# An encoder's softmax heads: VectorE scales the last head of every second group and adds it to the third, and residual additions move behind the maximum

## The chip, the core and the metric

The kernel runs on one core of a Trainium2 chip. A core has four engines that matter here, each with its own in-order queue of instructions: TensorE (PE in the profile; its weight loads are PEld), VectorE (DVE), ScalarE (ACT) and GpSimd (POOL). A fifth, SyncE (SP), issues most DMA transfers. Matrix products and transposes land in PSUM, from which VectorE and ScalarE read. Engines wait for each other through semaphores. The metric is the device time of one execution in microseconds.

## What is computed

The reference chains four blocks over a sequence of 2 batches x 1024 positions x 128 features, each with a layer norm before it and a residual addition behind it: a Mamba block, a mixture of experts, a six-layer encoder, and a feed-forward block with FP4 rounding. The change touches the encoder alone. One of its layers:

```python
scores = jnp.einsum('blhd,bmhd->bhlm', q, k) * inv_sqrt_d      # 16 heads of size 8
w_avg = jax.nn.softmax(scores, axis=-1).mean(axis=1)           # mean over the heads
new_w = jax.nn.softmax(CSCALE * w_avg + rel[None], axis=-1)    # second softmax
sa = jnp.einsum('blm,bme->ble', new_w, h)
h1 = _ln(h + sa, l1w, l1b)
h2 = _ln(h1, l2w, l2b)
ff = jax.nn.relu(h2 @ w1.T + b1_) @ w2.T + b2_
return (_ln(h2 + ff, l3w, l3b), None)
```

For each block of 128 query rows, sixteen softmax matrices of 128 x 1024 are averaged. Since the average is a sum, the heads may be added in any order and by any engine.

## The kernel before

The encoder does 6 layers x 2 batches x 8 blocks of 128 rows x 16 heads = 1536 steps, one head of one row block each. The method run (L1067) writes the order of all four engines' instructions by hand, step by step; no scheduler moves them. In step s it issues, in this order:

- release (L1098): if a piece of feed-forward work has a result waiting in PSUM, the instruction that takes it out (on ScalarE, or for the second feed-forward product the addition L926 on VectorE);
- in one step of sixteen, residual (L1057): VectorE takes a reciprocal of the second softmax's sum (L1062) and adds the mixed values to the layer's input (L1063). Every fourth such residual also puts the layer's norms, feed-forward and next projection (between, L885) on the list of work, in pieces;
- scores (L947): PE computes 128 x 1024 scores in two matmuls (L963) into PSUM, and VectorE takes their negated maximum (L966);
- in one step of four, scaled (L981): VectorE takes the reciprocals of four heads' softmax sums (L986), and GpSimd multiplies each of the four heads' exponentials by its reciprocal, in place in SBUF (L989), one instruction of 128 x 1024 a head;
- added (L991): for a group of four heads whose scores were issued ten steps before, PE transposes scaled exponentials onto two accumulators in PSUM (L1008). A group takes four steps: two heads' first halves, the other two heads' first halves, and then the same for the second halves. Each step is eight transposes of 128 x 128, and PSUM adds them up over the 16 heads;
- in two steps of sixteen, shifted (L1018) adds the distance term to the mean on VectorE (L1022), and second (L1032) takes its exponential on ScalarE (L1035);
- exponentials (L969): ScalarE takes the head's exponential and its sum (L972), from PSUM into one of 13 SBUF tiles;
- in one step of sixteen, mixed (L1043): PE multiplies the second softmax with the layer's input (L1048). In the other steps one piece of the listed work is issued.

Scores, the mixed values and all feed-forward results share three PSUM buffers (L668, L706). A score matmul can start when ScalarE has taken the exponential of an earlier user of its buffer. VectorE meets its instructions strictly in the order above: a maximum cannot start while an instruction issued ahead of it waits.

The GpSimd queue holds the scalings and, between them, products and additions of layer norms (L781 to L805), the addition L900, and the splitting of queries and keys into bfloat16 parts (L847, L849).

Of the kernel before, what the change touches and what calls it, by code (L numbers as in the profile page):

```python
# [14 lines left out]
ALU = mybir.AluOpType  # L15
# [13 lines left out]
NL, NH, DH, FF = 6, 16, 8, 512  # L29
# [605 lines left out]
class Encoder:  # L635
# [345 lines left out]
    def scaled(self, a, s):  # L981

        nc = self.nc
        m, hh = divmod(s, NH)
        rz = self.small.tile([P, self.GT], F32, tag="rz", bufs=4, name=f"rz_{a['who']}_{s}")
        nc.vector.reciprocal(rz, a["z", m][:, hh : hh + self.GT])  # L986
        for i in range(self.GT):
            e = a["e", s + i]
            nc.gpsimd.tensor_scalar(e, e, rz[:, i : i + 1], 1.0, ALU.mult, ALU.mult)  # L989

    def added(self, a, s, i):  # L991

        m, hh = divmod(s, NH)
        if hh == 0 and i == 0:
            a["acc", m] = [
                self.psa.tile([P, 4, P], F32, tag=f"acc{k}", name=f"acc_{a['who']}_{m}_{k}")
                for k in range(2)
            ]  # L1000
        half, two = divmod(i, 2)
        for j in (2 * two, 2 * two + 1):
            e = a["e", s + j]
            if half:
                del a["e", s + j]
            for n in range(4):
                at = (4 * half + n) * P
                self.nc.tensor.matmul(  # L1008
                    a["acc", m][half][:, 3 - n, :],
                    e[:, at : at + P],  # L1010
                    self.c.ident,
                    is_transpose=True,
                    start=hh + j == 0 and n == 0,
                    stop=hh + j == NH - 1,
                    skip_group_check=True,
                )

# [49 lines left out]
    def run(self):  # L1067
        th = self.TH
        drain(self.layer(0))
        for b in range(B):  # L1070
            self.hn[b] = self.hidden(b, f"in_{b}")
            for half in range(2):
                hs = slice(half * th, half * th + th)
                src = self.x[:, b * TB : (b + 1) * TB, :][:, hs, :]
                drain(self.norm(self.hn[b][:, hs, :D], src, f"c0_{b}_{half}"))
        for half in range(2):
            drain(self.project(0, 0, half))
        steps = TB * NH
        n = NL * B * steps
        lag, gt = self.LAG, self.GT  # L1080
        atts = {}
        work = []

        def add(b, pieces):
            work.append([b, pieces, None])

        def advance(i):

            if i >= len(work):
                return False  # L1090
            try:
                work[i][2] = next(work[i][1])
                return work[i][2] is not WAIT
            except StopIteration:
                del work[i]
                return False

        def release():  # L1098

            for i in range(len(work)):  # L1100
                if work[i][2] is HOLD:
                    advance(i)
                    return

        def of(s):
            return atts[s // steps], s % steps

        for half in range(2):
            add(1, self.project(0, 1, half))
        for s in range(n + lag + gt + 6):  # L1110
            release()

            t = s - lag - gt - 4
            if t >= 0 and t % NH == NH - gt:
                a, ts = of(t)
                m = ts // NH
                self.residual(a, m)
                if m % th == th - 1:
                    add(a["b"], self.between(a["l"], a["b"], m // th))
            if s < n:  # L1120
                if s % steps == 0:
                    i = s // steps
                    while any(b == i % B for b, _, _ in work):
                        advance(0)
                    atts[i] = self.begin(i)
                    if i % B == B - 1 and i // B + 1 < NL:
                        work.insert(0, [None, self.layer(i // B + 1), None])
                self.scores(*of(s))
            if s % gt == 1 and gt < s <= n + 1:
                self.scaled(*of(s - gt - 1))  # L1130
            t, i = divmod(s - lag, gt)
            t *= gt
            last = 0 <= t < n and t % NH == NH - gt and i % 2
            if 0 <= t < n:
                self.added(*of(t), i)
                if last:
                    a, ts = of(t)
                    self.shifted(a, ts // NH, i // 2)
            if s < n:
                self.exponentials(*of(s))  # L1140
            if last:
                self.second(a, ts // NH, i // 2)
            t = s - lag - gt - 3
            if t >= 0 and t % NH == NH - gt:
                a, ts = of(t)
                self.mixed(a, ts // NH)
            else:
                first = 1 if s % 4 == 3 and len(work) > 1 else 0
                if not advance(first):
                    advance(1 - first)  # L1150
        while work:
            advance(0)


def drain(pieces):
    for _ in pieces:
        pass
# [190 lines left out]
```

## Time and profile before

Three runs took 3608.43, 3609.01 and 3609.79 us (median 3609.01).

| | us |
|---|---|
| time of the profiled execution | 3610.56 |
| its span, first to last instruction | 3608.5 |
| PE busy | 3077.6 (85%) |
| VectorE busy | 2652.2 (73%) |
| ScalarE busy | 2494.5 (69%) |
| GpSimd busy | 2520.3 (70%) |
| the encoder's heads, first to last maximum | 669 to 3384 |
| mean granted TensorE clock | 0.917 of full speed |

How to read the lines that follow. A group's line names source line, engine, operation, the tiles written and read, the shape and the count; behind the first bar come busy time in us and the mean length of one instruction in ns; behind the second the idle time of the engine just ahead of these instructions, and what ended most of it. A line of the timeline has the start in us, the length in us, engine, source line, tiles, shape and how many instructions it merges; square brackets hold idle time ahead of it. A line of a window has start and end, the length, and the busy time of PE, PEld, VectorE, ScalarE and GpSimd in it, with instruction counts in brackets, then the granted clock, the DMA share and GB/s. Since PE's instructions are pipelined and their ends are modelled, start-to-start times say more about PE than its busy time.

### The profile page before, as it was taken

What the parts mean: (1) busy time and instruction counts of PE and PEld (TensorE: products, weight loads), DVE (VectorE), ACT (ScalarE), POOL (GpSimd) and SP (SyncE); (2) the same over time, 40 slices, a digit from 0 to 9 for tenths busy, and PEclk for the clock granted to TensorE, in tenths of its full rate; (3) what the DMA queues carried; (4) which work ended last, traced back from release to release, by engine and by line L of the source; (5) the groups of instructions that cost most, each with busy time, mean ns of one, the idle gap of its engine ahead of it and who ended that gap; (6) DMA issues with size and microseconds to landing.
All of it is one profiled execution on the core that took longest, in us unless ns stands there. A gap on an engine that the chain in (4) does not pass through costs nothing. (4 is left out here: it accounts for less than half of the span.)

```text
span 3608.5 us, 56501 instructions
## 1 busy us (share of the span) xinstructions
PE 3077.6 (85%) x20551; PEld 2409.3 (67%) x20551; DVE 2652.2 (73%) x4250; ACT 2494.5 (69%) x4506; POOL 2520.3 (70%) x2791
## 2 busy tenths in 40 slices
PE   5656997688999999899999999999999999999735
PEld 2345664376777777777777777777777777777513
DVE  6887434476887787787877778877778777778488
ACT  4553334476888888777887777877788777878532
POOL 3997001666887888777887778877788777877532
PEclk8656998799999999999999999999999999999856
DMA  2453001311111121111201111111111111110000
GB/s 80 116 133 90 1 1 26 81 14 23 35 29 36 20 51 22 30 39 16 49 24 29 35 20 42 31 30 33 21 40 27 25 35 20 38 18 8 1 7 11
DMA packets 124043, 125.09 MB, mean 35 GB/s; under 512 B 13459, under 2 KB 102372, under 8 KB 120308
## 3 DMA queue, kind: packets, MB, share of 16 engines
q1 hardware_dynamic: 122900, 118.82, 15.7%
q8 instruction: 162, 2.65, 0.3%
q0 software_dynamic: 864, 2.66, 0.2%
q14 instruction: 117, 0.96, 0.1%
HBM read 101.25 MB, written 20.19 MB: 34 GB/s over the span
## 5 line engine op out<-in xcount | busy, mean ns | idle before, releaser
L966 DVE TENSOR_REDUCE nm<-sc 128x1 f32<-128x1024 f32 x1536 | 1851.6, 1218 | 433.4 <-PE sc L963 394.5
L972 ACT ACTIVATE e<-sc,nm 128x1024 f32<-128x1024 f32 x1536 | 1703.9, 1112 | 521.5 <-DVE nm L966 380.7
L989 POOL TENSOR_SCALAR e<-e,rz 128x1024 f32<-128x1024 f32 x1536 | 1690.6, 1120 | 504.9 <-DVE rz L986 461.2
L1008 PEld LDWEIGHTS acc<-ident,e 128*128 128x128 f32 x12288 | 1465.1, 142 | 344.1 <-POOL e L989 35.3
L1008 PE MATMUL acc<-ident,e 128*128 128x128 f32 x12288 | 1636.3, 276 | 14.9 <-POOL e L989 14.9
L963 PE MATMUL sc<-k,q 72*128 72x512 bf16 x3072 | 939.5, 387 | 164.9 <-ACT e L972 112.4
L963 PEld LDWEIGHTS <-q 72*128 72x128 bf16 x3072 | 305.5, 100 | 299.5 <-issue 272.1
L972 ACT ACTIVATION_READ_ACCUMULATOR e<-sc,nm 128x1 f32 x1536 | 297.8, 194 | 0.0
L286 PE MATMUL ys<-ident,yc 128*128 128x128 f32 x512 | 113.3, 382 | 105.8 <-POOL yc L418 88.5
L581 ACT ACTIVATE hT<-ph,b 128x512 f32<-128x512 f32 x128 | 88.0, 687 | 135.9 <-PE ph L574 133.6
L286 PEld LDWEIGHTS ys<-ident,yc 128*128 128x128 f32 x512 | 84.4, 196 | 142.3 <-POOL yc L418 107.2
L615 POOL TENSOR_TENSOR x<-fo,x 128x512 f32<-128x512 f32 x4 | 5.1, 1278 | 235.6 <-DVE fo L94 235.6
L598 DVE SCALAR_TENSOR_TENSOR eo<-po,hot,eo 128x128 f32<-128x128 f32 x256 | 71.9, 344 | 132.7 <-PE po L590 127.4
L1048 PE MATMUL sa<-h,prT 128*128 128x129 f32 x1280 | 161.6, 280 | 8.6 <-ACT e L972 7.3
L1048 PEld LDWEIGHTS sa<-h,prT 128*128 128x128 f32 x1280 | 153.6, 195 | 11.9 <-ACT e L972 11.1
L369 POOL TENSOR_TENSOR db<-dtx,bb 128x512 f32<-128x512 f32 x128 | 159.6, 1266 | 0.2
L590 PEld LDWEIGHTS po<-m_w,hT 128*128 128x128 f32 x1024 | 125.1, 195 | 30.6 <-ACT hT L581 15.7
L1035 ACT ACTIVATE prT<-mean,zero 128x512 f32<-128x512 f32 x192 | 137.0, 714 | 8.2 <-DVE mean L1022 8.2
L356 ACT ACTIVATE da<-dt,zero,na 128x512 f32<-128x512 f32 x128 | 99.8, 781 | 55.0 <-DVE hh L402 51.3
L1022 DVE SCALAR_TENSOR_TENSOR mean<-acc,rel 128x512 f32<-128x512 f32 x192 | 128.8, 671 | 11.6 <-PE acc L1008 11.5
L590 PE MATMUL po<-m_w,hT 128*128 128x128 f32 x1024 | 127.3, 278 | 0.0
L793 ACT ACTIVATE r<-r,v_c,r_c 128x128 f32<-128x128 f32 x192 | 83.4, 484 | 47.3 <-POOL v_c L788 47.3
(313 smaller groups left out, 2808.9 us busy)
## 6 DMA issues: line engine op xcount, KB each, us to landing
bb<-bcd SPq DMA_DIRECT2D x128, 256.0 KB
q<-d_bq SPq DMA_DIRECT2D x432, 64.0 KB
k<-d_bk SPq DMA_DIRECT2D x144, 192.0 KB
d_bq<-part_bq SPq DMA_DIRECT2D x72, 128.0 KB
d_bk<-part_bk SPq DMA_DIRECT2D x72, 128.0 KB
e_W<-in_L_attn_W SPq DMA_DIRECT2D x12, 256.0 KB
m_w<-in_L_ffn_W POOLq DMA_DIRECT2D x2, 1024.0 KB, 11.0
e_ln_w<-in_L_attn_ln_w SPq DMA_DIRECT2D x18, 64.0 KB
```

Of the source, the lines that this page charges most:

```text
L286: nc.tensor.matmul(ys[k][:, t, :], src[:, t * P : (t + 1) * P], c.ident, is_transpose=True, start=first and t == 0, stop=last, skip_group_ ...
L356: nc.scalar.activation(da[g, k], dt[b][:, k, halves[h]], AF.Exp, bias=c.zero, scale=na[:, k, j : j + 1],)
L369: nc.gpsimd.tensor_mul(db[g, k], dtx[b][:, k, halves[h]], bb[g][:, 0, :])
L590: nc.tensor.matmul(po[:, m, :], hT[:, k, m * P : (m + 1) * P], t["w2"][:, e, k, :], start=k == 0, stop=k == NHC - 1,)
L963: nc.tensor.matmul(sc[:, ss], q, qk["kt"][hh // self.GH][:, hh % self.GH, ss], start=True, stop=True)
L966: nc.vector.tensor_reduce(a["nm", m][:, hh : hh + 1], sc, AX.X, ALU.max, negate=True)
L972: self.nc.scalar.activation(e, a.pop(("sc", s)), AF.Exp, bias=a["nm", m][:, hh : hh + 1], accum_out=a["z", m][:, hh : hh + 1],)
L989: nc.gpsimd.tensor_scalar(e, e, rz[:, i : i + 1], 1.0, ALU.mult, ALU.mult)
L1008: self.nc.tensor.matmul(a["acc", m][half][:, 3 - n, :], e[:, at : at + P], self.c.ident, is_transpose=True, start=hh + j == 0 and n == 0, ...
L1022: self.nc.vector.scalar_tensor_tensor(t, a["acc", m][half].rearrange("p n q -> p (n q)"), 1.0 / NH, self.rel[:, at : at + self.HL], ALU.mu ...
L1035: self.nc.scalar.activation(t.rearrange("p n q -> p (n q)"), a.pop(("mean", m, half)), AF.Exp, bias=self.c.zero,)
L1048: self.nc.tensor.matmul(sa[:, : D + 1], prT[n // 4][:, 3 - n % 4, :], a["h"][:, n, :], start=n == 0, stop=n == TB - 1,)
```

## The change

In every second group of four heads, GpSimd scales only three heads, in the order third, first, second. Two steps after the group's reciprocals, VectorE multiplies the fourth head's exponentials by its reciprocal and adds them to the third head's scaled exponentials, in place: one scalar_tensor_tensor of 128 x 1024 with both tensors in SBUF. PE then transposes three heads of that group instead of four, so the group's second and fourth steps have four transposes each instead of eight.

Besides, release and the residual move from the head of the step to behind the scores, so on VectorE they stand behind the step's maximum; what puts the next work on the list is one step later than before.

```diff
-        for i in range(self.GT):
+        heads = [0, 1, 2, 3]
+        if self.merges(s):
+            heads = [2, 0, 1]
+            a["rz", s] = rz
+        for i in heads:
             e = a["e", s + i]
             nc.gpsimd.tensor_scalar(e, e, rz[:, i : i + 1], 1.0, ALU.mult, ALU.mult)
+
+    def merges(self, s):
+        return s // self.GT % 2 == 1
+
+    def merged(self, a, s):
+        if self.merges(s):
+            e = a["e", s + 2]
+            self.nc.vector.scalar_tensor_tensor(
+                e, a.pop(("e", s + 3)), a.pop(("rz", s))[:, 3:4], e, ALU.mult, ALU.add
+            )
...
-        for j in (2 * two, 2 * two + 1):
+        n_heads = self.GT - self.merges(s)
+        for j in range(2 * two, min(2 * two + 2, n_heads)):
...
-                    stop=hh + j == NH - 1,
+                    stop=hh + self.GT == NH and j == n_heads - 1,
...
         for s in range(n + lag + gt + 6):
-            release()
-
-            t = s - lag - gt - 4
+            t = s - lag - gt - 5
             if t >= 0 and t % NH == NH - gt:
                 a, ts = of(t)
                 m = ts // NH
-                self.residual(a, m)
                 if m % th == th - 1:
                     add(a["b"], self.between(a["l"], a["b"], m // th))
...
                 self.scores(*of(s))
+            release()
+            t = s - lag - gt - 4
+            if t >= 0 and t % NH == NH - gt:
+                a, ts = of(t)
+                self.residual(a, ts // NH)
             if s % gt == 1 and gt < s <= n + 1:
                 self.scaled(*of(s - gt - 1))
+            if s % gt == 3 and gt < s <= n + 3:
+                self.merged(*of(s - gt - 3))
```

## The prediction

> **What bounds the kernel now.** I read the page's busy table first, then the stretch in which the encoder's heads run (from the first maximum to the last), then the groups.
>
> ```profile
> span 3608.5 us, 56501 instructions
> ...
> 669.00:3384.00 2715.00, 2518.72 (x18036) 2040.55 (x18035) 2112.20 (x2943) 2143.67 (x3865) 2149.15 (x2407) 0.97 0.15 29
> ```
>
> The second line has start and length of the stretch, then busy time of PE, PEld, DVE, ACT and POOL, the granted clock, the DMA share and GB/s. The reader is to see that the encoder is three quarters of the span, that PE is busy 93% of it, and DVE, ACT and POOL each 78 to 79%.
>
> ```profile
> L966 DVE TENSOR_REDUCE nm<-sc 128x1 f32<-128x1024 f32 x1536 | 1851.6, 1218 | 433.4 <-PE sc L963 394.5
> ...
> L989 POOL TENSOR_SCALAR e<-e,rz 128x1024 f32<-128x1024 f32 x1536 | 1690.6, 1120 | 504.9 <-DVE rz L986 461.2
> L1008 PEld LDWEIGHTS acc<-ident,e 128*128 128x128 f32 x12288 | 1465.1, 142 | 344.1 <-POOL e L989 35.3
> L1008 PE MATMUL acc<-ident,e 128*128 128x128 f32 x12288 | 1636.3, 276 | 14.9 <-POOL e L989 14.9
> ```
>
> VectorE's main idle time is waiting for PE's scores. Next the timeline of PE, in a calm place, gives a head's true price there:
>
> ```profile
> 1848.79 1.04 PE L1008 MATMUL acc<-ident,e 128*128 128x128 f32 x8
> 1849.67 0.60 PE L963 MATMUL sc<-k,q 72*128 72x512 bf16 x2
> 1850.10 1.04 PE L1008 MATMUL acc<-ident,e 128*128 128x128 f32 x8
> ```
>
> From score to score is 1.31 us, of which eight transposes hold 0.88 (1849.67 - 1848.79), so 0.11 each. VectorE's maxima behind each other start 1.13 us apart (two of them took 2.36 us at 1857.11, one 1.22). So PE leads VectorE by only 0.18 us a head in calm places; it is the clear bound only where feed-forward matmuls lie between the heads. Busy time by row of 16 heads shows this (columns as above; four rows are one half of a batch's layer, 64 heads):
>
> ```profile
> 1792.86:1818.33 25.47, 24.58 (x190) 20.68 (x189) 22.16 (x34) 21.64 (x43) 18.92 (x23) 1.00 0.37 63
> 1818.33:1845.07 26.74, 25.21 (x184) 20.19 (x183) 21.39 (x32) 22.21 (x41) 23.52 (x24) 1.00 0.06 20
> 1845.07:1870.88 25.81, 23.65 (x178) 19.30 (x177) 22.20 (x32) 21.68 (x38) 24.79 (x30) 1.00 0.15 35
> 1870.88:1903.80 32.92, 29.60 (x198) 23.30 (x197) 21.83 (x26) 25.54 (x46) 23.68 (x27) 0.95 0.01 3
> ```
>
> VectorE's idle time (length less busy) is 3.31, 5.35, 3.61 and 11.09 us. Over the encoder it is (2715.0 - 2112.2) / 96 rows = 6.28, against 5.84 here, so I scale by 1.075: 4.4 us in each of three light rows, about 11.9 in the heavy one.
>
> **The change part by part, for a row of 16 heads (96 rows).**
>
> *TensorE, removed.* Two groups of four lose one head's transposes: 16 x 0.11 = 1.76 us; 169 us over the kernel if PE alone set the pace. By the mean of the group's busy time (1636.3 / 12288 = 0.133) it would be 204 us, the upper bound of any gain; the lower is nothing, where VectorE sets the pace. I take 0.11, which is start to start.
>
> *GpSimd, removed.* 192 scalings of 1.120 us, 215 us. Its idle time is (2715.0 - 2149.2) / 96 = 5.9 us a row, and what waits for it on PE's side is 14.9 + 35.3 us in all, so this alone buys little. The order in the group becomes third, first, second head; PE reads the group's first two heads five heads after the reciprocal was issued, so 1.12 us of delay is hidden by about 8 us.
>
> *VectorE, added.* 192 scalar_tensor_tensor of 128x1024 with both tensors in SBUF. The same shape runs in the Mamba stage (L220 below) in 1.279 us. The bounds are 1.19 (instructions behind each other overlap by 0.09) and 1.285 (the longest of twelve). I take 1.28: 246 us, 2.56 a row. Per head the engine is then near PE: PE's 1.31 x 8 - 0.88 = 9.6 us for eight calm heads, VectorE's 1.13 x 8 + 1.2 + 0.2 for two reciprocals = 10.4.
>
> *VectorE, the wait that the merge adds.* It is issued two maxima behind the group's reciprocal, and needs only the third head's scaling, which GpSimd does first. But GpSimd is then in its second or third scaling. What the trace shows of VectorE reading two SBUF tensors beside a busy GpSimd:
>
> ```profile
> L220 DVE SCALAR_TENSOR_TENSOR cv<-xp,cw,cv x12: 1276/1279/1285, 40.2 to 58.3; 128x1024 f32<-128x1024 f32 x12
> ...
> L274 DVE SCALAR_TENSOR_TENSOR w<-w,u x8: 692/1596/5852, 66.7 to 198.5; 128x512 f32<-128x512 f32 x8
> ...
> L275 DVE SCALAR_TENSOR_TENSOR w<-ps_dt,w x8: 691/691/692, 67.5 to 200.1; 128x512 f32<-128x512 f32 x8
> ...
> 91.20 2.50 POOL L369 TENSOR_TENSOR db<-dtx,bb 128x512 f32<-128x512 f32 x2
> ...
> 92.05 5.85 DVE L274 SCALAR_TENSOR_TENSOR w<-w,u 128x512 f32<-128x512 f32 x1
> ...
> 93.65 1.26 POOL L418 TENSOR_TENSOR yc<-hh,bb 128x512 f32<-128x512 f32 x1
> ...
> 94.87 2.48 POOL L369 TENSOR_TENSOR db<-dtx,bb 128x512 f32<-128x512 f32 x2
> ```
>
> L274 (minimum, median, maximum in ns) and L275 are the same operation and size; only L274 has both tensors in SBUF. L275 always takes 0.69 us, L274 up to 5.85: in the last rows it ends 0.55 us after GpSimd's unbroken run ends at 97.35. In the encoder no VectorE instruction reads two SBUF tensors today (L1022, L1063 and L926 take one from PSUM), so the wait is new. Its bounds are 0 (GpSimd idle, or no exclusion against a one-input scaling) and 5852 - 692 = 5.16 us. For the value I took, in the trace, each second group's reciprocal, the end of the second maximum behind it and the end of the third scaling, which would be GpSimd's last. The scaling ends later in 75% of 191 groups; quartiles of the difference are 0.16, 0.77 and 1.62 us; counting an earlier end as 0, the mean is 1.26. When both start at once it is plain arithmetic: two maxima take 2.5 us, three scalings 3.4. I take 1.2. Other GpSimd work behind the run (layer norm products of 1.27 us, L803 and L805) can lengthen it; a GpSimd one scaling shorter in eight shortens it.
>
> The Trainium skill, page "SBUF — State Buffer", section "Who interferes with whom", speaks against this change: a VectorE instruction with two SBUF inputs and a GpSimd instruction that reads SBUF exclude each other for the whole instruction, and whichever issued first goes on. L274 agrees in kind. Read as a wait for the running scaling only, it would be an estimate of half of 1.12, 0.56 us a merge, and the sum below would come out 16 us faster than before. The rows of L274 show longer waits, through four instruction boundaries, so I keep 1.2.
>
> Queued behind the waiting merge on VectorE is the next head's maximum; ACT's exponential (L972) waits for that, and PE's score three allocations on waits for ACT, since the scores have three PSUM buffers. TensorE's wait for the merged head itself is hidden: it is read four heads later, about 6.5 us.
>
> *Moved.* The residual (L1062, 169 ns, and L1063, 351) and the feed-forward additions (L926, 292 ns) go behind the maximum. Before, they fell into the 0.6 us in which PE makes the next scores, so VectorE lost little; now they follow the maximum and the next may start up to 0.5 us later, 96 x 0.5 + 96 x 0.3 = 77 us if nothing hides it. Below nothing: the maximum need no longer wait behind L1062's 133.8 us of waiting, at most that. I take 0, because where VectorE lags, order leaves its sum as it is. The evacuations on ACT stay between the same exponentials. The feed-forward pieces, GpSimd work and DMA issues on SP included, start one head later; a batch's layer has 128 heads, so I count nothing. GpSimd's and SP's queues gain nothing else.
>
> *Sum.* A row asks VectorE for 2 x (1.28 + 1.2) = 4.96 us more. I let 1.0 us of idle stay (the wait at the row's mixing matmul, about 1.5 us, is partly used). Light row: 4.96 - (4.4 - 1.0) = +1.56. Heavy row: the merge fits, and PE's 1.76 is gained, less some for its first calm heads: -1.2. Four rows: 3 x 1.56 - 1.2 = +3.48; 24 such fours: +84 us. On the profiled execution's own 3610.56 us (span 3608.5 and 2.1 around it) that is 3694; the median is 1.55 lower, so 3693.
>
> **The rivals.**
> *Faster: no wait.* If GpSimd's scaling, with one input, does not exclude the merge, or leaves it in at a boundary, w = 0: light rows 2.56 - 3.4 = -0.84, heavy -1.76, 24 x -4.28 = -103, 3506 us. With w the light row is 2.56 + 2w - 3.4, and with -1.5 in the heavy row the sum is zero at w = 0.67 us; that decides. For it: all eight waits of L274 are against two-input instructions. Against: 75% of the runs end too late.
> *Much slower: the merge waits until GpSimd has emptied its queue*, layer norm products included: w = 2.5, light rows 7.56 - 3.4 = +4.16, heavy 7.56 - 10.9 < 0, say -0.5: 24 x 12 = +288, 3897 us. For it: the 5.85. Against: in three of L274's eight, VectorE got in between two instructions.
> *No change:* w near 0.67, 3609.
>
> **How the numbers follow.** Forecast 55% (3630 to 3790 its own range, w from 0.8 to 1.7), faster rival 25%, much slower 15%, no change 5%. The measurement can tell about 0.2%, 7 us. Below 3545 lies about half of the faster rival, above 3830 half of the much slower: a fifth in all. So faster 0.25, same 0.05, slower 0.70.
>
> **What would show it.** Merges with a mean over 2 us and a spread up to 4 or more, ending about 1.3 us after a GpSimd run's end; GpSimd's idle time up, PE's too; calm rows near 27.5 us, heavy ones shorter by about 1. Merges at 1.28 throughout would prove me wrong, as would light rows that stay at 26 with merges near 2.5: then VectorE's idle time was more usable than I think.

## The result and the profile after

The changed kernel takes 3742.36 us (median of 4 runs, 3739.87 to 3743.40) against 3608.72: a ratio of 1.0370, 95% interval 1.0352 to 1.0388. The change costs 134 us. The forecast was 3693 us, 84 slower.

The page of the changed kernel, its first line, and the stretch of the encoder's heads (start and end, length, busy time of PE, PEld, VectorE, ScalarE and GpSimd, granted clock, DMA share, GB/s):

```profile
span 3738.2 us, 53054 instructions
...
668.30:3514.40 2846.10, 2486.41 (x16513) 1905.67 (x16512) 2353.85 (x3134) 2149.37 (x3865) 2036.14 (x2215) 0.96 0.15 28
```

The encoder takes 2846 us instead of 2715; the rest of the kernel is as long as before. TensorE is busy 32 us less, GpSimd 113 less, VectorE 242 more. TensorE's share falls from 93 to 87%; VectorE's rises from 78 to 83%. No engine is full: each now waits more for the others. The page's groups say who waits (busy time and mean length, then idle time and what ended it, as in the prediction):

```profile
L966 DVE TENSOR_REDUCE nm<-sc 128x1 f32<-128x1024 f32 x1536 | 1828.5, 1212 | 467.7 <-PE sc L963 462.7
L972 ACT ACTIVATE e<-sc,nm 128x1024 f32<-128x1024 f32 x1536 | 1705.1, 1112 | 682.4 <-DVE nm L966 561.2
L993 POOL TENSOR_SCALAR e<-e,rz 128x1024 f32<-128x1024 f32 x1344 | 1550.6, 1171 | 743.9 <-DVE rz L986 715.0
...
L1024 PE MATMUL acc<-ident,e 128*128 128x128 f32 x10752 | 1484.6, 279 | 21.4 <-POOL e L993 21.4
```

ScalarE's wait for the maxima has grown from 381 to 561 us. VectorE's own wait for the scores, instead of shrinking, has grown from 395 to 463. Both fit one loop: scores, maximum, exponential, and the exponential frees the PSUM buffer for a later score. In the list of waits, TensorE's scores waiting for ScalarE rise from 112 to 241 us. The same four rows of 16 heads as in the prediction:

```profile
1857.63:1887.59 29.96, 25.20 (x183) 19.84 (x182) 25.33 (x36) 22.29 (x43) 17.93 (x23) 1.00 0.30 54
1887.59:1917.52 29.93, 26.06 (x171) 19.24 (x170) 24.89 (x35) 22.18 (x39) 22.38 (x21) 0.94 0.06 19
1917.52:1946.84 29.32, 25.56 (x164) 19.54 (x162) 24.91 (x36) 21.35 (x38) 23.04 (x27) 0.88 0.18 30
1946.84:1979.35 32.51, 28.34 (x179) 20.91 (x178) 24.13 (x27) 24.95 (x46) 22.79 (x26) 0.95 0.01 3
```

The three light rows are 3.2 to 4.5 us longer than before, the heavy one 0.4 shorter. VectorE's idle time in the light rows is 4.63, 5.04 and 4.41 us, where it was 3.31, 5.35 and 3.61. So in these light rows the merges were simply added; they did not fill idle time. In the heavy row it falls from 11.09 to 8.38, and there a part of them fits.

The merge itself, as all its instructions and as one of them on the timelines of VectorE and GpSimd:

```profile
L1002 DVE SCALAR_TENSOR_TENSOR e<-e,rz,e x192: 1270/1607/2235, 691.4 to 3518.4; 128x1024 f32<-128x1024 f32 x192
...
1799.21 2.33 DVE L966 TENSOR_REDUCE nm<-sc 128x1 f32<-128x1024 f32 x2
1801.87 2.14 DVE L1002 SCALAR_TENSOR_TENSOR e<-e,rz,e 128x1024 f32<-128x1024 f32 x1 [0.33 <-POOL e L993]
1803.93 2.34 DVE L966 TENSOR_REDUCE nm<-sc 128x1 f32<-128x1024 f32 x2
...
1800.71 4.28 POOL L993 TENSOR_SCALAR e<-e,rz 128x1024 f32<-128x1024 f32 x3
1804.96 1.27 POOL L803 TENSOR_TENSOR r<-r,e_ln_w 128x512 f32<-128x512 f32 x1
```

A third of the merges take 1.27 to 1.28 us; the median is 1.61, the longest 2.24, the mean 1.66. The one shown starts as the first scaling ends and the second begins, and takes 2.14. The three scalings beside it take 4.28 us, where three behind each other took 3.31 before: the third ends about a microsecond late, behind the merge. Over the kernel 72 scalings take over 1.2 us, and all 1344 together 71 us more than at 1.118 each.

### The profile page after: what moved, and what is told of

Read it like the earlier page. It is cut to its first block, busy times and chain, and to the rows that moved or that the text cites. A ratio compares the mean times of both kernels' runs of the same rounds, so it can differ in the third digit from the quotient of the medians.

```text
span 3738.2 us, 53054 instructions
## 1 busy us (share of the span) xinstructions
PE 3045.2 (81%) x19015; PEld 2275.7 (61%) x19015; DVE 2892.5 (77%) x4442; ACT 2500.1 (67%) x4506; POOL 2408.0 (64%) x2599
## 5 line engine op out<-in xcount | busy, mean ns | idle before, releaser
L966 DVE TENSOR_REDUCE nm<-sc 128x1 f32<-128x1024 f32 x1536 | 1828.5, 1212 | 467.7 <-PE sc L963 462.7
L993 POOL TENSOR_SCALAR e<-e,rz 128x1024 f32<-128x1024 f32 x1344 | 1550.6, 1171 | 743.9 <-DVE rz L986 715.0
L1024 PEld LDWEIGHTS acc<-ident,e 128*128 128x128 f32 x10752 | 1317.5, 144 | 350.0 <-issue 36.6
L1024 PE MATMUL acc<-ident,e 128*128 128x128 f32 x10752 | 1484.6, 279 | 21.4 <-POOL e L993 21.4
L963 PE MATMUL sc<-k,q 72*128 72x512 bf16 x3072 | 954.9, 393 | 317.3 <-ACT e L972 241.2
L1002 DVE SCALAR_TENSOR_TENSOR e<-e,rz,e 128x1024 f32<-128x1024 f32 x192 | 318.6, 1659 | 42.8 <-POOL e L993 42.8
L1064 PE MATMUL sa<-h,prT 128*128 128x129 f32 x1280 | 170.0, 289 | 6.5 <-ACT e L972 6.0
L1064 PEld LDWEIGHTS sa<-h,prT 128*128 128x128 f32 x1280 | 161.5, 204 | 11.1 <-ACT e L972 10.2
```

The costliest lines, as they stand in the source:

```text
L963: nc.tensor.matmul(sc[:, ss], q, qk["kt"][hh // self.GH][:, hh % self.GH, ss], start=True, stop=True)
L966: nc.vector.tensor_reduce(a["nm", m][:, hh : hh + 1], sc, AX.X, ALU.max, negate=True)
L1002: self.nc.vector.scalar_tensor_tensor(e, a.pop(("e", s + 3)), a.pop(("rz", s))[:, 3:4], e, ALU.mult, ALU.add)
L1024: self.nc.tensor.matmul(a["acc", m][half][:, 3 - n, :], e[:, at : at + P], self.c.ident, is_transpose=True, start=hh + j == 0 and n == 0, ...
L1064: self.nc.tensor.matmul(sa[:, : D + 1], prT[n // 4][:, 3 - n % 4, :], a["h"][:, n, :], start=n == 0, stop=n == TB - 1,)
```

## The experiments

All runs were timed in three rounds against the kernel before on the same chip (its medians 3606 to 3608 us); the ratio follows each time.

**The two halves of the change, apart.** Merge alone, with release and residual where they were (the edit against the changed kernel, the removed lines of the moved order left out):

```diff
-            t = s - lag - gt - 5
+            release()
+            t = s - lag - gt - 4
...
+                self.residual(a, m)
```

> The merge as in the changed kernel, but release and residual at the head of the step as before. If the merge makes the loss and the moved order costs nothing (the forecast's own term), 3742 us within 10. If the moved order costs the 77 us that the forecast named as its upper bound, about 3665. If it helps where VectorE is late, 3750 or more.

Measured: 3679.90 us, 1.0198 (1.0180 to 1.0216), so 72 us for the merge alone. The moved order alone, with four scalings and no merge (against the kernel before):

```diff
         for s in range(n + lag + gt + 6):
-            release()
-            t = s - lag - gt - 4
+            t = s - lag - gt - 5
...
-                self.residual(a, m)
...
                 self.scores(*of(s))
+            release()
+            t = s - lag - gt - 4
+            if t >= 0 and t % NH == NH - gt:
+                a, ts = of(t)
+                self.residual(a, ts // NH)
```

> The moved order alone, no merge. Forecast's term: 3609 us within 8. If the residual behind the maximum holds up the next maximum: up to 77 more, 3686. If together with the previous run the two parts don't add up to 134, the order matters only where VectorE is loaded.

Measured: 3644.93 us, 1.0104 (1.0083 to 1.0124), 37 us. The forecast had put the move at nothing. Together the parts give 109 of 134 us: the move costs 62 us beside the merge.

**What the merge's time is made of.** First with the moved order: a maximum over one SBUF tile in place of the merge, and nothing in its place. Both leave the fourth head of every second group out of the result.

```diff
-            self.nc.vector.scalar_tensor_tensor(
-                e, a.pop(("e", s + 3)), a.pop(("rz", s))[:, 3:4], e, ALU.mult, ALU.add
-            )
+            a.pop(("e", s + 3)), a.pop(("rz", s))
+            t = self.small.tile([P, 1], F32, tag="mx", name=f"mx_{a['who']}_{s}")
+            self.nc.vector.tensor_reduce(t, e, AX.X, ALU.max)
```

> The merge is replaced by a maximum over the third head's scaled tile (one SBUF input, about 1.2 us), so VectorE is as long busy and waits for the same scaling, but reads no second SBUF tensor; the fourth head of every second group is left out of the result. If the shared-port wait makes the loss (192 x 0.38 us on VectorE plus about 71 us on GpSimd), at most 3742 - 73 = 3669, and no scaling over 1.2 us. If VectorE's plain time makes it, above 3700.

Measured: 3651.77 us, 1.0119 (1.0104 to 1.0134), 91 us under the changed kernel. With nothing in its place (only the first added line above stays):

> The merge is left out altogether (the fourth head of every second group is missing from the result): the savings of TensorE and GpSimd alone. If TensorE sets the pace everywhere, 3609 - 169 = 3440 us. If VectorE is close behind in the light rows (0.18 us a head), three light rows gain about 0.7 us and the heavy one 1.76, some 90 us: 3520.

Measured: 3583.79 us, 0.9928 (0.9911 to 0.9945). Both values of the expectation, 3440 and 3520, lay lower. TensorE's and GpSimd's savings bring 61 us against the moved order alone; VectorE's plain time costs 68, more than they bring, and the merge costs 91 more than a maximum of nearly the same length. The same two kernels in the old order:

> No merge, fourth head of every second group missing from the result, order and start of the listed work as in the kernel before. If the savings of TensorE and GpSimd are worth the same as with the moved order (3645 - 3584 = 61 us), 3607 - 61 = 3546 us. If the later start hid part of them, 3500 to 3530; the forecast's term for four rows with no VectorE cost and 1 us of idle kept (PE's saving alone) was 1.76 us a row where PE sets the pace.

Measured: 3508.39 us, 0.9731 (0.9702 to 0.9759). The savings are worth 97 us there, of the 169 that TensorE's start-to-start times would give if it set the pace alone; the moved order had hidden over a third of the 97.

> A maximum over the third head's tile in place of the merge (fourth head missing from the result), order and start as before. If port wait and VectorE's plain time simply add and don't depend on the order: 3680 - 90 = 3590 us, and 3546 + 68 = 3614 from the other side; a value between 3590 and 3614 closes the sum. Under 3570 or over 3640 the parts depend on each other.

Measured: 3586.52 us, 0.9948 (0.9933 to 0.9964), just under the 3590 that the sum gave from one side. So VectorE's plain time takes back 78 us, and the merge costs 93 more than the maximum. The lines behind this verdict are those of the scalings (minimum, median, maximum in ns), first with the merge alone, then with the maximum in its place:

```profile
L993 POOL TENSOR_SCALAR e<-e,rz x1344: 1107/1118/2204, 680.4 to 3452.2; 128x1024 f32<-128x1024 f32 x192
```

```profile
L993 POOL TENSOR_SCALAR e<-e,rz x1344: 1111/1122/1148, 678.8 to 3367.4; 128x1024 f32<-128x1024 f32 x192
```

and that of the maximum, in the page's columns (busy time, mean, idle time ahead):

```profile
L1004 DVE TENSOR_REDUCE mx<-e 128x1 f32<-128x1024 f32 x192 | 232.7, 1212 | 36.6 <-POOL e L993 36.6
```

The two VectorE instructions stand in the same place and wait for the same scaling (36.6 us in all here, 46.5 with the merge). Where VectorE reads one SBUF tensor, it takes 1.21 us and no scaling is over 1.15; where it reads two, it takes 1.67 on average and scalings reach 2.20. That the two engines keep each other out is shown.

The merge differs from the maximum in two more ways: it writes a whole tile to SBUF, and TensorE reads what it writes. Neither explains the long merges. The trace of the merge alone has another scalar_tensor_tensor that writes SBUF, the one of the distance term, with one of its tensors in PSUM:

```profile
L1038 DVE SCALAR_TENSOR_TENSOR mean<-acc,rel x192: 650/672/691, 712.2 to 3458.1; 128x512 f32<-128x512 f32 x192
```

156 of these 192 run while a scaling does, and none takes over 0.691 us. And no wait in that trace is put down to the merge's result. How the 93 us divide is not shown: they hold up to 13 us of plain length (192 x (1.28 - 1.21)), the rest of the merges' waits on VectorE, the held-up scalings on GpSimd, and perhaps a lower clock of TensorE (last section).

**Other places for the merge,** in the old order. Two heads later, directly ahead of the next group's reciprocal, for which GpSimd waits (against the changed kernel; the lines that restore the old order are left out):

```diff
+            if s % gt == 1 and 2 * gt < s <= n + 5:
+                self.merged(*of(s - gt - 5))
             if s % gt == 1 and gt < s <= n + 1:
                 self.scaled(*of(s - gt - 1))
-            if s % gt == 3 and gt < s <= n + 3:
-                self.merged(*of(s - gt - 3))
```

> The merge alone (order and start as before), two steps later, directly ahead of the next group's reciprocal, when GpSimd is mostly idle and can't start the next scalings. If the port wait makes 70 to 90 us, merges near 1.28 us and about 3680 - 75 = 3605. If VectorE's plain time in the light rows decides, 3660 to 3680.

Measured: 3645.39 us, 1.0106 (1.0089 to 1.0122).

```profile
L1002 DVE SCALAR_TENSOR_TENSOR e<-e,rz,e x192: 1262/1276/2186, 692.9 to 3414.2; 128x1024 f32<-128x1024 f32 x192
```

The median merge is down to 1.276 us, and 17 scalings instead of 74 are held up; the time falls by 34 us, not by 75. The place ends most of the mutual wait, but the merge now stands ahead of the reciprocal that the scalings need, and it still costs VectorE's plain time. In the lists of waits TensorE waits 93 us for scalings, where it was 55 with the merge alone, and ScalarE 24 instead of 1; what each is worth was not separated. Of the two merges a row, the next run keeps only the one in the step of the mixing matmul:

```diff
-        return s // self.GT % 2 == 1
+        return s // self.GT % 4 == 1
```

> As the run with the merge ahead of the reciprocal, but only the one merge a row that falls in the step of the mixing matmul, where VectorE waits 1.5 to 2 us for TensorE anyway. If VectorE's time is free there, it costs nothing and TensorE saves 0.88 us a row, of which light rows use 0.2 to 0.4: 3570 to 3600. If not, 3609 or more.

Measured: 3586.12 us, 0.9948 (0.9932 to 0.9964): 20 us faster than the kernel before. The 59 us between these two runs are the net cost of adding the row's other merge. That this one falls into a wait of VectorE's is in the list of waits, at the reciprocal of the residual, first before, then here:

```profile
DVE rz L1062 <- PE sa L1048: 133.8, 94, 3.8
```

```profile
DVE rz L1078 <- PE sa L1064: 24.5, 65, 2.6
```

And the same with the merge behind the group's reciprocal (against the run just shown):

```diff
-            if s % gt == 1 and 2 * gt < s <= n + 5:
-                self.merged(*of(s - gt - 5))
             if s % gt == 1 and gt < s <= n + 1:
                 self.scaled(*of(s - gt - 1))
+            if s % gt == 1 and 2 * gt < s <= n + 5:
+                self.merged(*of(s - gt - 5))
```

> The one merge a row in the step of the mixing matmul, but behind the group's reciprocal, so that GpSimd's scalings have just started. If only the port wait differs: merges near 1.28 + 0.8 us, 96 x 0.8 = 77 us of VectorE time that the mixing wait partly hides: 3586 to 3630. If the reciprocal's earlier start is worth more than the wait: 3575 to 3586.

Measured: 3584.07 us, 0.9936 (0.9915 to 0.9958), the same within the intervals. Its merges and scalings:

```profile
L1002 DVE SCALAR_TENSOR_TENSOR e<-e,rz,e x96: 1251/1256/2247, 694.6 to 3356.9; 128x1024 f32<-128x1024 f32 x96
...
L993 POOL TENSOR_SCALAR e<-e,rz x1440: 1111/1122/2094, 682.1 to 3368.5; 128x1024 f32<-128x1024 f32 x180
```

I expected long merges here and they did not come. VectorE goes straight from the reciprocal to the merge and gets in first, so the scalings wait: 77 of them take over 1.2 us, against 7 with the merge ahead of the reciprocal. The time shows no cost; that GpSimd has room for it there is my reading. So a merge that falls into a wait of VectorE's is worth having, and both of these beat both kernels.

**What in the move costs.** First only the later start of the listed work (against the kernel before):

```diff
                 self.residual(a, m)
+            t = s - lag - gt - 5
+            if t >= 0 and t % NH == NH - gt:
+                a, ts = of(t)
+                m = ts // NH
                 if m % th == th - 1:
                     add(a["b"], self.between(a["l"], a["b"], m // th))
```

> The kernel before with one change: the norms, feed-forward and projection are put on the list of work one step later; residual and additions stay ahead of the maximum. If the 37 us of the moved order alone come from this shift (GpSimd's second norm product now falls behind a group's four scalings, and VectorE's statistics wait for it with the maxima behind them), about 3609 + 30 = 3640 us. If they come from the residual behind the maximum, 3609 within 8.

Measured: 3640.23 us, 1.0094 (1.0077 to 1.0110). For the order alone, release, residual and the listing of the work all stand behind the scores, with the old index t = s - lag - gt - 4:

> The kernel before with residual, release and additions behind the maximum, but the listed work starts in the same step as before. Shift theory: 3609 within 12. Order theory (96 x 0.5 + 96 x 0.3 us at most): 3640 to 3686.

Measured: 3624.39 us, 1.0056 (1.0041 to 1.0071), 18 us: above one expectation, below the other. Both parts cost, and alone the later start costs more. They do not add up: 34 and 18 alone, 37 together. The mechanism of the later start on the timelines, first GpSimd before:

```profile
1741.92 3.31 POOL L989 TENSOR_SCALAR e<-e,rz 128x1024 f32<-128x1024 f32 x3
1745.18 1.29 POOL L803 TENSOR_TENSOR r<-r,e_ln_w 128x512 f32<-128x512 f32 x1
1746.55 1.28 POOL L805 TENSOR_TENSOR r<-r,e_ln_b 128x512 f32<-128x512 f32 x1
1747.81 5.49 POOL L989 TENSOR_SCALAR e<-e,rz 128x1024 f32<-128x1024 f32 x5
```

then GpSimd and VectorE at the same place with the moved order alone:

```profile
1770.16 1.28 POOL L803 TENSOR_TENSOR r<-r,e_ln_w 128x512 f32<-128x512 f32 x1
1771.41 4.42 POOL L989 TENSOR_SCALAR e<-e,rz 128x1024 f32<-128x1024 f32 x4
1775.79 1.28 POOL L805 TENSOR_TENSOR r<-r,e_ln_b 128x512 f32<-128x512 f32 x1
...
1777.10 0.49 DVE L767 BATCH_NORM_STATS2 st_c<-r 128x6 f32<-128x128 f32 x2 [3.78 <-POOL r L805]
1777.50 1.21 DVE L966 TENSOR_REDUCE nm<-sc 128x1 f32<-128x1024 f32 x1
```

One step later, the layer norm's second product (L805) is issued behind a group's scalings instead of ahead of them, and 4.4 us pass. The statistics (L767) wait for it on VectorE, and the next maximum stands behind them for 3.78 us. VectorE's wait of this kind, in us, times and longest, is before and with the later start alone:

```profile
DVE st_c L767 <- POOL r L805: 33.7, 11, 7.0
```

```profile
DVE st_c L767 <- POOL r L805: 69.8, 20, 7.0
```

That is 36 us more, for a loss of 34.

The last run restores the start in the changed kernel:

> The changed kernel with one thing undone: the listed work starts in the same step as in the kernel before; residual and additions stay behind the maximum. The moved order and start together cost 3742 - 3680 = 62 us beside the merge. If the later start makes most of it, as it does alone (34 of 37 us), 3695 to 3710; if the residual behind the maximum makes it where VectorE is loaded, 3725 to 3742.

Measured: 3722.35 us, 1.0328 (1.0308 to 1.0348). The time lies just under the range for the order and above that for the start: here the start is worth 20 us and the order 42, more than the 18 it cost alone. For the start the same wait fits again: 16.7 us in this run and 37.0 in the changed kernel, 20 us more. For the order, the waits of VectorE with the merge alone, in us, times and longest:

```profile
DVE nm L966 <- PE sc L963: 291.6, 273, 50.3
...
DVE rz L1078 <- PE sa L1064: 62.4, 52, 3.6
DVE r L926 <- PE ps_f L918: 47.0, 65, 16.4
```

and with merge and order, early start:

```profile
DVE nm L966 <- PE sc L963: 459.5, 416, 50.0
...
DVE r L926 <- PE ps_f L918: 17.9, 4, 15.8
...
DVE rz L1078 <- PE sa L1064: 2.0, 1, 2.0
```

I read this as follows. In the old order VectorE did the residuals and additions while TensorE made the next scores. Behind the maximum, it waits for the scores with nothing to do (168 us more, 90 less at the other two lines), and then has that work still ahead of it. The cost of the order is measured; this mechanism rests on the waits alone.

## Why the prediction came out as it did

The sum, as the runs in the old order build it up (ratio x 3608 us): savings of TensorE and GpSimd -97; VectorE's plain time +78; the second SBUF tensor +90, with up to 13 of plain length in it; together +71 for the merge (72 by the medians). Residuals and additions behind the maximum +47; the later start +15. Total +133.

- *Direction and cause: right.* The merge loses because VectorE's time and its exclusion against GpSimd outweigh TensorE's savings. The merge alone cost 72 us; the sum had 84, and this was the whole of it. By rows the picture is less exact than it looks: over 17 of the 24 fours, light rows grew by 1.92, 3.34 and 1.19 us (predicted 1.56) and the heavy one shrank by 1.16 (predicted 1.2), but that is with the moved order. With the merge alone the same rows change by +1.31, +1.96, -0.76 and -0.41 us: one light row gains, and the heavy row much less than predicted. Its agreement was luck.
- *"I take 0" for the moved instructions: wrong; 62 us.* This term is more than the whole miss of 50, since the merge came out 12 below its 84. "Where VectorE lags, order leaves its sum as it is" fails because VectorE does not lag all the time: at the mixing matmul, and wherever a feed-forward product has to be taken out, it waits in each row, and the residual was work for that wait. The bound that I had written, 77 us, held for it (42 to 47). The later start I dismissed by counting heads (128 in a batch's layer); what counts is the order on GpSimd's queue.
- *The wait, w = 1.2 us: too large.* Merges take 0.38 us over 1.28, and the semaphore wait for the first scaling adds 42.8 / 192 = 0.22: 0.60 in all. The sign that I had named, a mean over 2 us and a spread up to 4, did not come: the mean is 1.66 and the longest 2.24. I had carried over from L274 that VectorE does not get in between GpSimd's instructions. Against the one-input scalings it does, at the next boundary: the longest merge is 0.96 us over the shortest. By the decision point that I gave (w = 0.67), the kernel should then have come out level.
- *"I let 1.0 us of idle stay": too small,* and this undid the error before it: that 84 came near 72 is partly luck. Light rows of the changed kernel keep 4.4 to 5.0 us of VectorE's idle time. The merge falls where VectorE is not idle, and the three PSUM buffers, as I read it, turn a delay of VectorE into a wait of TensorE, which VectorE then shares. That last link rests on the lists of waits (112 to 241 us); no run changed the number of buffers.
- *GpSimd alone buys little:* no run took GpSimd's saving apart from TensorE's. The exclusion took back 71 of the 215 us that GpSimd saved.
- *The rivals.* "No wait" falls: scalings and merges do exclude each other. "Until GpSimd has emptied its queue" falls too: it is one instruction. The rule that I weighed, of the Trainium skill's page "SBUF — State Buffer", section "Who interferes with whom", read as a wait for the running instruction, gave an estimate of 0.56 us a merge; the merges show 0.38 on average. Of the 192, 130 are longer than 1.29 us, and these are held up by 0.56 us on average: the estimate was right for a merge that meets a scaling, and a third met none. So a wait for the running instruction was nearer than my reading of L274. Of L274's eight, only six were held up; why they, against two-input instructions, waited through as many as four boundaries is still open.

## What to carry to other kernels

Idle time of an engine is not room for new work unless the work falls where the engine waits. Ask of each insertion point what ends the wait there: one merge a row in the mixing matmul's step gained 20 us, a second one elsewhere in the row lost 59. And treat "only moved" instructions as a cost: work that filled a wait leaves a hole there, and a piece that starts one step later can land behind a long run on one engine's in-order queue, and hold up another.

## What the runs showed of the hardware that was not expected

Between a VectorE instruction with two SBUF inputs and a queue of GpSimd scalings, the one that is ready first goes, and the other waits for one instruction: with the merge directly behind the reciprocal, the 96 merges had a median of 1.256 us and 77 scalings were held up; two heads later, the 192 merges had a median of 1.61 and 72 scalings were held up. In these two traces no merge was more than 1.0 us over the shortest, less than the 1.118 of one scaling.

The granted clock in the encoder was 0.98 with the maximum in place of the merge (old order), 0.97 before and 0.96 with the merge alone, although TensorE had the same 16510 matmuls in the first and the last of these; its busy time there was 2406.5 and 2435.5 us. The cause was not tested, so a part of the 93 us may be TensorE's slower clock.
